# Splitting each 256-column product of the value phase into two of 128 columns

## The chip, the core and the metric

The kernel runs on one core of one Trainium2 chip. The metric is the time on the device in microseconds: the kernel before takes 3204.21 us, the median of three runs from 3204.08 to 3205.99. A difference of under 0.2% (6.4 us) counts here as no difference.

The core's engines work side by side, each with its own list of instructions: TensorE (PE in the profile) multiplies matrices, VectorE (DVE) and ScalarE (ACT) work on elements, GpSimd (POOL) and SyncE (SP) mostly start transfers. TensorE's work shows in two rows of the profile: a weight load (PEld) puts the stationary operand, here called the stationary block, into the array, and a matmul (PE) streams the moving operand past it. Results go to PSUM, memory beside the array in banks of 512 fp32 columns.

## The reference

Two attention blocks, one after the other, on a batch of 8 images of 512 channels and 32 x 32 positions (1024 tokens). All is fp32. One block, cut to what matters:

```python
xn  = group_norm(x, 8 groups) * gamma + beta
qkv = einsum('oc,bchw->bohw', qkv_w, xn) + qkv_b     # q, k, v: 512 channels each
attn = softmax(einsum('bhds,bhdt->bhst', q, k) * scale)   # 8 heads of 64
out = einsum('bhst,bhdt->bhds', attn, v)
x = x + einsum('oc,bchw->bohw', proj_w, out) + proj_b
```

The second block is the same with other weights. The change is in how `v` is computed.

## The kernel before, in words

The work is cut into 16 jobs: one image in one layer each. The images are taken in pairs, so that the two layers of an image are not neighbours. A job has four stages on TensorE, and the stages of neighbouring jobs are laced into one order that the kernel writes out itself (PE, ACT and DVE keep the order in which the Python code issues instructions; side work is issued by `later(delay, fn)` when a counted time, moved on by `advance(us)`, has come; this counted time is a plan, and nothing on the chip waits for it):

- **Value phase** (`v_phase`, line 482). It makes `v` with tokens on partitions. The 512 x 512 by 512 x 1024 product is done as one level of a seven-product scheme: the operands are cut into 2 x 2 blocks, sums and differences of blocks are formed (`tx` on the data side, `FACTOR` on the weight side), and seven block products replace eight. Each block product is 256 input channels by 512 tokens by 256 output channels.
- **Deep phases** (`deep_phases`, line 574). The output projection of the job before, then `k` and `q` of this job, with two levels of the scheme, 49 small products each, issued at line 636.
- **Attention** (`Attention`, line 858). 64 steps per job; each computes scores (line 878) and the product of the exponentials with `v` (line 909). Both address the array in quarters of 64 x 64.
- Group norm of a later job is laced in on ACT and DVE.

Inside the value phase, `group(i)` is called for `i` in 0 and 1: each takes half of the 512 tokens of a block product, that is two tiles `ti` of 128 tokens, and has four PSUM banks of its own (`z`, `y`, `u`, `v`). A bank holds two token tiles side by side, 256 output channels each. The function `one` (line 491) issues one product: the stationary block is a 128-channel by 128-token piece of the data, the moving operand is 256 columns of one weight block `w`. `product` calls it for two token tiles `ti` and two halves `cc` of the 256 input channels, so that a block product for one `i` is four calls. The second `cc` adds to the first in PSUM. `chain` (line 431) runs after each block product what empties or copies banks: `scalar.copy` at lines 438, 442, 518 and 522, `tensor_add` at line 520. `half_phase` issues all seven block products for `i` = 0 and 1 by turns. Only for the first job, `begin` issues the first half of some products earlier, between the steps of group norm; there, tiny products of one column (`averages` at line 329 and `variance` at line 341, for the group norm's statistics) stand between the products of line 494.

Per job this makes 7 x 2 x 2 x 2 = 56 calls of `one`; over 16 jobs, 896. In the trace each call stands as two passes, that is two weight loads and two matmul records of the same shape: 112 of each per job, 1792 of each in all. The same holds for every fp32 product of the kernel.

Of the flags: a product with `start` set begins an accumulation afresh; it is set only for the first product of a bank (`ti == 0`, `cc == 0`).

Of the kernel before, what the change touches and what calls it, by code (L numbers as in the profile page):

```python
# [19 lines left out]
P = 128  # L20
# [17 lines left out]
CH = C // 2  # L38
# [34 lines left out]
def fast_path(  # L73
# [10 lines left out]
    nc = tc.nc  # L84
# [8 lines left out]
    ps, turns = {}, [0]  # L93
# [116 lines left out]
    def wide(w):  # L210
        return w.rearrange("p a b -> p (a b)")[:, : 2 * CH].rearrange("p (cc o) -> p cc o", cc=2)
# [165 lines left out]
    xn, tx, to = [None], [None], [None]  # L377
# [15 lines left out]
    def right(src, t, o):  # L393

        if o in (4, 5, 6):
            return t[:, {5: 0, 6: 1, 4: 2}[o]]
        rows = 0 if o in (1, 7) else 2
        cols = slice(0, HALF) if o in (1, 2) else slice(HALF, S)
        return src[:, rows : rows + 2, cols]
# [54 lines left out]
    def half_phase(n, which, group, order):  # L454

        steps = []
        begins.clear()
        for i in range(2):
            by = {b: bank(i, b, f"{b}_{which}_{n}_{i}") for b in ("zyuv", "uvzy")[i]}
            product, put5, put, begin = group(i)  # L460
            steps.append(chain(product, put5, put, *(by[b] for b in "zyuv")))
            at = {1: by["z"], 5: by["v"], 2: by["y"]}
            begins.append(lambda o, begin=begin, at=at: begin(o, at[o]))
        thunks = []
        for o in order:
            key = (n, which, o)
            turns = (1, 0) if o == order[-1] and n > 0 else (0, 1)

            def first(o=o, i=turns[0]):
                steps[i](o)  # L470
                advance(1.72)

            def second(o=o, key=key, i=turns[1]):
                steps[i](o)
                if key in held:
                    used(key)
                advance(1.72)

            thunks += [first, second]
        return thunks  # L480

    def v_phase(n, order, first=None):
        vt[0] = acts.tile([P, NT, C], F32, tag="v", name=f"v_{n}")
        dst, src = vt[0], xn[0]

        def group(i):
            s5 = epool.tile([P, 2, HALF], F32, tag="e", name=f"s5_{n}_{i}")[:, 0, :]

            begun = []

            def one(o, ps, ti, cc, start):
                w = first[:, FACTOR[o]] if first is not None else wide(held[n, V, o])
                t0 = (2 * i + ti) * P
                nc.tensor.matmul(  # L494
                    ps[:, ti * CH : (ti + 1) * CH],
                    right(src, tx[0], o)[:, cc, t0 : t0 + P], w[:, cc, :],
                    start=(start and ti == 0 and cc == 0), stop=(cc == 1),
                    skip_group_check=True,
                )

            def begin(o, ps):
                one(o, ps, begun.count(o), 0, o in (1, 5))
                begun.append(o)

            def product(o, ps, start):
                for ti in range(2):
                    for cc in range(2):
                        if cc == 1 or o not in begun:
                            one(o, ps, ti, cc, start)

            def tokens(ps):
                return ps.rearrange("p (t c) -> p t c", t=2)

            def put(oh, sh, ps):
                t0 = sh * NT // 2 + 2 * i
                to_ = dst[:, t0 : t0 + 2, oh * CH : (oh + 1) * CH]
                if sh == 0:
                    nc.scalar.copy(to_, tokens(ps))  # L518
                else:
                    nc.vector.tensor_add(to_, tokens(ps), tokens(s5))  # L520

            return product, lambda ps: nc.scalar.copy(s5, ps), put, begin

        return half_phase(n, V, group, order)
# [253 lines left out]
    def last_weights(n):  # L778
        w = acts.tile([P, NW, 2, CH], F32, tag="deep", name="w_last")
        nc.sync.dma_start(w, factors[O, jobs[n][1]])  # L780
        return w
# [502 lines left out]
    for n in range(-1, len(jobs)):  # L1284
        last = n + 1 == len(jobs)
        outs = None
        if n >= 0:
# [7 lines left out]
            if last:  # L1295
                w = last_weights(n)
# [311 lines left out]
```

## Time and profile before

| What | Value |
|---|---|
| Median of three runs | 3204.21 us |
| Span of the profiled execution, first to last instruction | 3202.4 us |
| TensorE matmul records | 22917, busy 3183.5 us (99%) |
| Weight loads | 22917, busy 1862.2 us (58%) |
| VectorE | 2773.9 us (87%) |
| ScalarE | 1914.3 us (60%) |
| Mean granted TensorE clock | 0.999 |
| One value phase, first to last matmul start (jobs 3 to 16) | 24.49 us |

The profile is of one execution on the chip. The span lies 1.8 us below the median of the runs, which is time before the first and after the last instruction and the scatter of one execution. A matmul's row runs from the moment it begins to read to a modelled end, and rows overlap: the distance from one start to the next, not the row's length, tells what a pass costs. In the listings, "x16" merges sixteen neighbouring records of one kind, with the start of the first.

### The profile page before, as it was taken

What the parts mean: (1) busy time and instruction counts of PE and PEld (TensorE: products, weight loads), DVE (VectorE), ACT (ScalarE), POOL (GpSimd) and SP (SyncE); (2) the same over time, 40 slices, a digit from 0 to 9 for tenths busy, and PEclk for the clock granted to TensorE, in tenths of its full rate; (3) what the DMA queues carried; (4) which work ended last, traced back from release to release, by engine and by line L of the source; (5) the groups of instructions that cost most, each with busy time, mean ns of one, the idle gap of its engine ahead of it and who ended that gap; (6) DMA issues with size and microseconds to landing.
All of it is one profiled execution on the core that took longest, in us unless ns stands there. A gap on an engine that the chain in (4) does not pass through costs nothing.

```text
span 3202.4 us, 57786 instructions
## 1 busy us (share of the span) xinstructions
PE 3183.5 (99%) x22917; PEld 1862.2 (58%) x22917; DVE 2773.9 (87%) x3990; ACT 1914.3 (60%) x3063; POOL 99.5 (3%) x94
## 2 busy tenths in 40 slices
PE   9999999999999999999999999999999999999999
PEld 7366384663836648366483754837547375573744
DVE  8897999979889798897988889888898888978878
ACT  4746646466565665656656565565656656566564
POOL 0000000000000000000000000000000000000000
PEclk9999999999999999999999999999999999999999
DMA  8234172350713315034170421504316051150611
GB/s 291 74 105 123 49 216 67 95 166 22 213 25 90 89 28 158 22 105 130 31 211 16 117 69 37 149 16 137 101 44 194 16 138 48 49 136 16 174 37 42
DMA packets 156726, 307.80 MB, mean 96 GB/s; under 512 B 34088, under 2 KB 60576, under 8 KB 156192
## 3 DMA queue, kind: packets, MB, share of 16 engines
q1 hardware_dynamic: 139856, 272.05, 26.6%
q0 software_dynamic: 16592, 31.99, 6.1%
q8 instruction: 181, 2.97, 0.4%
q14 instruction: 97, 0.79, 0.1%
HBM read 225.13 MB, written 45.68 MB: 85 GB/s over the span
## 4 chain that ended last, share of the span: by engine, by line
PE 94%; DVE 5%; DMA 1%; issue 0%; ACT 0%; POOL 0%; DVEq 0%; SPq 0%; ACTq 0%; POOLq 0%
PE sc L878 27%; PE po L909 27%; PE zd L636 10%; PE vd L636 10%; PE z L494 6%; PE yd L636 5%; PE ud L636 4%; PE v L494 2%; PE y L494 2%; PE u L494 1%; DVE acc L895 1%; PE z_last L822 0%; DMA x<-p 0%; DMA w<-deep 0%; DVE w L156 0%
## 5 line engine op out<-in xcount | busy, mean ns | idle before, releaser
L883 ACT ACTIVATE e<-sc 128x1024 f32<-128x1024 f32 x1024 | 1045.0, 1024 | 563.6 <-PE sc L878 456.2
L878 PE MATMUL sc<-q,k 64*64 64x512 f32 x8192 | 1058.2, 589 | 0.0
L909 PE MATMUL po<-e,v 64*64 64x512 f32 x8192 | 1057.3, 589 | 0.0
L895 DVE TENSOR_TENSOR acc<-acc,e 128x1024 f32<-128x1024 f32 x768 | 936.2, 1219 | 58.7 <-ACT e L883 12.1
L909 PEld LDWEIGHTS po<-e,v 64*64 64x64 f32 x8192 | 313.2, 133 | 565.7 <-issue 552.9
L878 PEld LDWEIGHTS sc<-q,k 64*64 64x64 f32 x8192 | 311.6, 133 | 562.3 <-issue 544.2
L893 DVE TENSOR_TENSOR acc<-e,e 128x1024 f32<-128x1024 f32 x128 | 156.4, 1222 | 112.2 <-ACT e L883 112.1
L636 PE MATMUL zd<-deep,w 128*128 128x256 f32 x860 | 240.9, 379 | 1.1 <-DVE p L653 0.6
L636 PE MATMUL vd<-deep,w 128*128 128x256 f32 x804 | 224.4, 380 | 4.4 <-ACT yd L438 2.3
L636 PEld LDWEIGHTS zd<-deep,w 128*128 128x128 f32 x860 | 163.1, 190 | 24.7 <-DVE p L653 1.5
L636 PEld LDWEIGHTS vd<-deep,w 128*128 128x128 f32 x804 | 152.3, 190 | 27.2 <-ACT yd L438 2.7
L925 DVE TRANSPOSE_TENSOR_REDUCE r<-acc 128x32 f32<-128x1024 f32 x128 | 158.5, 1238 | 0.6
L682 POOL DMA_DIRECT2D x<-p x61 | 73.4, 1203 | 1974.0 <-ACT p L646 1408.5
L636 PE MATMUL vd<-os,w 128*128 128x256 f32 x420 | 118.2, 380 | 1.6 <-DVE p L655 1.5
L668 DVE TENSOR_TENSOR p<-p,p 128x1024 f32<-128x1024 f32 x94 | 114.2, 1215 | 0.0
L494 PE MATMUL z<-w,t 128*128 128x256 f32 x480 | 110.9, 379 | 0.0
L494 PE MATMUL z<-w,xn 128*128 128x256 f32 x480 | 110.1, 382 | 0.0
L518 ACT COPY v<-z 128x512 f32<-128x512 f32 x32 | 18.8, 586 | 148.7 <-PE z L494 148.7
L494 PEld LDWEIGHTS z<-w,xn 128*128 128x128 f32 x480 | 90.0, 190 | 23.8 <-issue 12.2
L442 ACT COPY ud<-zd 128x256 f32<-128x256 f32 x156 | 55.7, 357 | 76.5 <-PE zd L636 75.5
L653 DVE TENSOR_TENSOR p<-vd,s 128x256 f32<-128x256 f32 x63 | 26.7, 424 | 85.6 <-PE vd L636 85.6
L657 ACT COPY s<-vd 128x256 f32<-128x256 f32 x156 | 58.2, 373 | 70.1 <-PE vd L636 70.1
(242 smaller groups left out, 4193.8 us busy)
## 6 DMA issues: line engine op xcount, KB each, us to landing
w<-deep SPq DMA_DIRECT2D x287, 448.0 KB, 3.6
x<-p POOLq DMA_DIRECT2D x61, 512.0 KB, 6.5
rb<-rd SPq DMA_DIRECT2D x96, 256.0 KB, 4.1
w<-keep SPq DMA_DIRECT2D x84, 256.0 KB, 2.7
deep<-w SPq DMA_DIRECT2D x42, 448.0 KB, 3.3
w<-wqkv_dram SPq DMA_DIRECT2D x57, 256.0 KB, 2.8
x<-x_dram SPq DMA_DIRECT2D x28, 512.0 KB, 6.2
out_dram<-x SPq DMA_DIRECT2D x28, 512.0 KB, 6.0
```

What stands on the lines that cost most here:

```text
L442: nc.scalar.copy(u, z)
L494: nc.tensor.matmul(ps[:, ti * CH : (ti + 1) * CH], right(src, tx[0], o)[:, cc, t0 : t0 + P], w[:, cc, :], start=(start and ti == 0 and cc ...
L636: nc.tensor.matmul(ps, lhs[:, FACTOR[i], :], moving[i], start=start, stop=True, skip_group_check=True,)
L657: return chain(product, lambda ps: nc.scalar.copy(s5, ps), put, z, y, u, w)
L668: outer.append(lambda: nc.vector.tensor_add(to_, a, b))
L682: nc.gpsimd.dma_start(to_, p(part), accum_op=ALU.add)
L878: nc.tensor.matmul(sc[h * HD : (h + 1) * HD, j, :], k[r, hp, k0 : k0 + HD], q[r, hp, sh * HALF : (sh + 1) * HALF], start=True, stop=True,)
L883: nc.scalar.activation(e, sc, AF.Exp, scale=SCALE)
L893: nc.vector.tensor_add(acc[g], self.es[i - 1], e)
L895: nc.vector.tensor_add(acc[g], acc[g], e)
L909: nc.tensor.matmul(po[g][j * HD : (j + 1) * HD, h, :], v[r, kc, d0 : d0 + HD], e[r, j, :], start=(kc == 0), stop=(kc == NT - 1),)
L925: nc.vector.tensor_reduce(self.r[:, 0, m, :], self.acc.pop(g).rearrange("p j (b e) -> p (j b) e", e=RP), AX.X, ALU.add, apply_transpose=True,)
```

## The change

In `one`, the call of line 494 becomes a loop over two parts. Each part uses the same stationary block and takes 128 of the 256 columns of `w`, and writes 128 of the 256 columns of the bank's half. The flag `start` is set only for part 0.

```diff
-                nc.tensor.matmul(
-                    ps[:, ti * CH : (ti + 1) * CH],
-                    right(src, tx[0], o)[:, cc, t0 : t0 + P], w[:, cc, :],
-                    start=(start and ti == 0 and cc == 0), stop=(cc == 1),
-                    skip_group_check=True,
-                )
+                for part in range(2):
+                    c0 = part * P
+                    nc.tensor.matmul(
+                        ps[:, ti * CH + c0 : ti * CH + c0 + P],
+                        right(src, tx[0], o)[:, cc, t0 : t0 + P], w[:, cc, c0 : c0 + P],
+                        start=(start and ti == 0 and cc == 0 and part == 0), stop=(cc == 1),
+                        skip_group_check=True,
+                    )
```

`P` is 128, `CH` is 256. Nothing else differs; `advance(1.72)` for each block product, which paces the side work, is as before.

## The prediction

> **What bounds the kernel now.** I read the page's engine totals first, then the chain that ended last, then the order of time inside one value phase, and last the few places where the trace holds matmuls shorter than 256 columns.
>
> ```profile
> span 3202.4 us, 57786 instructions
> PE 3183.5 (99%) x22917; PEld 1862.2 (58%) x22917; DVE 2773.9 (87%) x3990; ACT 1914.3 (60%) x3063; POOL 99.5 (3%) x94
> ...
> PEclk9999999999999999999999999999999999999999
> ...
> PE 94%; DVE 5%; DMA 1%; issue 0%; ACT 0%; POOL 0%; DVEq 0%; SPq 0%; ACTq 0%; POOLq 0%
> ...
> L494 PE MATMUL z<-w,t 128*128 128x256 f32 x480 | 110.9, 379 | 0.0
> L494 PE MATMUL z<-w,xn 128*128 128x256 f32 x480 | 110.1, 382 | 0.0
> ...
> L494 PEld LDWEIGHTS z<-w,xn 128*128 128x128 f32 x480 | 90.0, 190 | 23.8 <-issue 12.2
> ```
>
> TensorE is busy from end to end at full clock and makes 94% of the chain, so any time added to its stream shows in full. The groups of line 494 have no idle time ahead of them. Loads equal matmuls in number (22917 each): every pass brings its own weight load. 190 ns is a load's row, 379 a matmul's, but both rows overlap their neighbours, so the cost must come from starts. The order of time in the third value phase, TensorE alone (start in us, row length in us, then the group):
>
> ```profile
> 398.72 3.62 PE L494 MATMUL v<-w,t 128*128 128x256 f32 x16
> 402.18 3.62 PE L494 MATMUL z<-w,t 128*128 128x256 f32 x16
> 405.63 3.62 PE L494 MATMUL y<-w,xn 128*128 128x256 f32 x16
> 409.08 3.62 PE L494 MATMUL z<-w,xn 128*128 128x256 f32 x16
> 412.54 3.62 PE L494 MATMUL u<-w,xn 128*128 128x256 f32 x16
> 415.99 1.89 PE L494 MATMUL z<-w,t 128*128 128x256 f32 x8
> ```
>
> Sixteen passes every 3.454 us: (415.99 - 398.72) / 80 = 215.9 ns a pass; the nanosecond records of the trace give 215.83. The view of waits, cut to this phase, has no TensorE wait. The phase is one unbroken stream, paced by the moving columns; each load starts 1 to 2 ns after the matmul before it and is hidden under that.
>
> What happens when the matmul is too short to hide the load shows only in the first job, where one-column products stand in the same stream:
>
> ```profile
> 15.47 0.28 PE L329 MATMUL pm<-mv,blk 128*128 128x1 f32 x2
> 15.61 1.11 PE L494 MATMUL v<-raw_v,t 128*128 128x256 f32 x4
> 16.56 0.28 PE L341 MATMUL pvar<-dev,blk 128*128 128x1 f32 x2
> 16.70 1.11 PE L494 MATMUL v<-raw_v,t 128*128 128x256 f32 x4
> 17.65 0.38 PE L1239 MATMUL first_u<-any 128*128 128x512 bf16 x1
> ```
>
> From 15.474 to 16.561 and on to 17.647 (the records' nanoseconds), each stretch holds two one-column passes and four of 256: 1.0865 us less 4 x 0.2158 leaves 223 ns, 111.6 ns for each short pass. A narrow cut shows the loads:
>
> ```profile
> 15.48 0.19 PEld L329 LDWEIGHTS pm<-mv,blk 128*128 128x128 f32 x1
> 15.59 0.30 PEld L494 LDWEIGHTS v<-raw_v,t 128*128 128x128 f32 x2
> ```
>
> In nanoseconds these loads start at 15.476, 15.586 and 15.697: 110 and 111 apart. The same distances at 12.4 and 16.6 us are 111 and 111, 110 and 112. So a pass which does nothing but bring its weights takes 110.8 (between loads) to 111.6 ns (between matmuls). That is the other pace of this engine.
>
> **What the Trainium skill says.** "TensorE: Matmul & The Clock Gate", section "Step-by-step: what each phase is for", says that the weights of the next tile load while the current matmul runs, into a background buffer. The trace agrees: 1 to 2 ns from matmul to load, and no lengthening of the 215.83 ns. Its section "LDWEIGHTS (loading the stationary operand)" prices a load at its columns over 1.2 GHz, 106.7 ns for 128; the trace's 110.8 is near, with the hand-off in it. Its section "Back-to-back issue gap" gives a bf16 matmul N/2.4 + 2.5 ns alone, but about 81 ns at N = 128 when each has its load, against 56 alone: 25 ns that overlap did not hide. No fp32 pair of 128 columns is in the trace before, so I keep this as the upper bound. "Perfetto Trace Analysis", section "Per-instruction lifecycle: what the profiler-reported window actually captures", says a TensorE row starts at prefetch and its end is estimated; hence starts alone are used here.
>
> **The change, part by part.** (1) Removed: 896 products, traced as 1792 passes at 215.83 ns. (2) Added: 1792 products, 3584 passes of 128 columns. Could the second part skip the load, its block being the same? The built program has full products, and in the trace before, the idle products of line 1130 use one block twice running and each pass still has its load. Besides, the two passes of one fp32 product sit between. I count 3584 loads.
>
> (3) Cost of a new pass, bounded from both sides. By columns: 256 columns take 215.83 ns; if 2.5 ns of it is fixed (the skill's figure), 128 take 106.7 + 2.5 = 109.2 ns. By load: 110.8 to 111.6. If both run side by side, as the first half of each matmul already does, the longer sets the pace: I take 111.0, inside the load's bounds. Two new passes cost 222.0 against 215.83: +6.2 ns for each old pass, x 1792 = +11.1 us, 0.69 us in each value phase. The lower end is 109.2: +2.6 x 1792 = +4.6 us. The upper end, 25 ns unhidden on 109.2, is 134: +52.6 x 1792 = +94 us.
>
> (4) Issue: a pair of load and matmul every 111 ns is an instruction per 55.5. Attention already does that for whole stages:
>
> ```profile
> 300.64 1.04 PE L878 MATMUL sc<-q,k 64*64 64x512 f32 x8
> 301.50 1.04 PE L909 MATMUL po<-e,v 64*64 64x512 f32 x8
> 302.36 1.04 PE L878 MATMUL sc<-q,k 64*64 64x512 f32 x8
> ```
>
> Eight matmuls and their eight loads every 0.86 us are 53.6 to 53.8 ns an instruction, so the sequencer keeps up. The margin is thin: the view proves this pace and no faster one.
>
> (5) Waits: the built program keeps the order of DVE, ACT, POOL and SP unchanged, and TensorE has 180 waiting products at this line before and after; no wait or signal is added. Nothing is moved past a queue. DMA: none. Behind TensorE, the copies at lines 438, 442, 518, 520 and 522 are released 0.1 us later per product; they wait for TensorE now (ACT for line 518 alone 185.4 us), so only the next TensorE stage matters, and it stands behind the same stream. DVE's side work in the phase (23.4 of 24.9 us busy) gets 0.7 us more room; if it were late, its cost would come at the deep phases, where TensorE waits 9 us in all today. One recovery: in the second value phase TensorE waits 1.2 us for the attention's last sum (line 932); the 24 old passes before it are slower now and take back 24 x 6.2 ns, 0.15 us. The first phase's half clock until 12.3 us doubles a handful of passes, both old and new. Sum: +11.0 us. Against the profiled span: 3202.4 + 11.0 = 3213.4; the 1.8 us that the median has over it stay: **3215.2 us**.
>
> **The rivals.**
> - *Column pace* (ends on the other side: no change). If the load's 1.6 ns start-up and hand-off vanish under a matmul of equal length, a pass is 109.2 ns: +4.6, 3208.8 us. For it: each path alone would fit. Against: one-column passes leave the load nothing to wait for and still pace at 111. It decides below (215.83 + 6.4/1.792) / 2 = 109.7 ns; above this the change is measurably slower.
> - *Partial exposure.* Load and matmul now end together, so a small hand-off that today has 105 ns of slack could show: 112.5 to 124 ns a pass, where 124 is two instructions at the 62 ns that the skill's clock-gate page ("Wait — 56ns, not 53.3ns?") gives for a software-decoded matmul. +16 to +58 us: 3221 to 3262. Against: attention's 53.6 ns per instruction and the even 110 to 112 chain.
> - *Load not hidden*, 134 ns: 3298 us. Against: today's loads are hidden wholly; for: the skill's 81 against 56.
> - *Load skipped*: even then columns pace at 109.2, the first rival's time. Nothing in the profile offers a gain above 0.2%, since all columns still stream; only a stage shifting by luck remains.
>
> **How the numbers follow.** Load pace (110 to 112.5 ns, 3210.6 to 3220): 0.60. Column pace, skipped load included: 0.16. Partial exposure: 0.14. Unhidden: 0.08. A gain: 0.02. The likeliest gives 3215.2. The range takes load and column pace (0.76) from 3207, and the lower half of partial exposure, to 3241 (0.83). 0.2%, 6.4 us, is what a measurement can tell: slower is 0.60 + 0.14 + 0.08 = 0.82, same 0.16, faster 0.02.
>
> **What would show it.** Right: 3584 loads at the line; starts in a value phase 110.5 to 111.5 ns apart, so a block product's row of 32 passes every 3.55 us and a phase of 25.1 to 25.2 us; weight loads nearly touching; no TensorE wait in the phase; attention and deep phases as before. Column pace: 3.49 us a block product. Exposure: 3.6 us and more. Wrong also if loads stay at 1792, if starts jitter (issue), or if TensorE waits grow in the deep phases.

## The result and the profile after

The changed kernel takes 3216.21 us, the median of five runs from 3215.82 to 3217.89, against 3204.21: a ratio of 1.0037 with a 95% interval of 1.0023 to 1.0051. Run again later with four runs of its own it came to 1.0052 (1.0035 to 1.0069). It is slower by some 12 to 16 us, against 11 forecast; both intervals lie above the 0.2% that counts as a difference.

The page of the kernel after, its totals, the line of the clock, the chain and two of the groups (busy us and mean ns behind the bar, then idle time):

```profile
span 3214.4 us, 61370 instructions
...
PE 3196.8 (99%) x24709; PEld 1926.0 (60%) x24709; DVE 2775.1 (86%) x3990; ACT 1912.8 (60%) x3063; POOL 99.5 (3%) x94
...
PEclk9999999999999999999999999999999999999999
...
PE 94%; DVE 4%; DMA 1%; issue 0%; SPq 0%; ACT 0%; DVEq 0%; ACTq 0%
...
L496 PEld LDWEIGHTS z<-w,xn 128*128 128x128 f32 x960 | 109.5, 192 | 12.2 <-issue 12.2
L496 PE MATMUL z<-w,t 128*128 128x128 f32 x960 | 114.5, 276 | 0.0
```

TensorE has 24709 matmuls and as many loads, 1792 of each more than before: no load was skipped. The span grew by 12.0 us and TensorE's busy time by 13.3; VectorE and ScalarE changed by at most 1.5 us. The chain is the same but for one per cent of VectorE. In the group of loads, the idle time was 23.8 us and is now 12.2, which is the one gap ahead of each phase, 0.76 us on average: the loads, which used to leave room between them, now follow each other without a break.

The order of time in the third value phase, TensorE alone:

```profile
398.30 3.74 PE L496 MATMUL v<-w,t 128*128 128x128 f32 x32
401.87 3.74 PE L496 MATMUL z<-w,t 128*128 128x128 f32 x32
405.44 3.74 PE L496 MATMUL y<-w,xn 128*128 128x128 f32 x32
409.02 3.74 PE L496 MATMUL z<-w,xn 128*128 128x128 f32 x32
412.59 3.74 PE L496 MATMUL u<-w,xn 128*128 128x128 f32 x32
416.17 1.95 PE L496 MATMUL z<-w,t 128*128 128x128 f32 x16
```

A block product took 3.454 us and takes 3.574: (416.17 - 398.30) / 160 = 111.7 ns a pass, 111.66 from the records' nanoseconds. From its first to its last matmul start the phase takes 25.43 us, against 24.49. No TensorE wait stands in it, as before. The busy time of the line's rows in this phase (stretch and its length, then TensorE, loads, clock, share of the DMA engines and GB/s), first of the kernel before, then of the kernel after:

```profile
395.10:419.70 24.60, 24.27 (x112) 21.20 (x112) 1.00 0.37 113
```

```profile
394.60:420.10 25.50, 25.21 (x224) 25.21 (x224) 1.00 0.34 109
```

Before, loads were busy for less time than matmuls; now both are busy for the same 25.21 us. From the sixth to the last job the period of a job is 197.85 us before and 198.69 after, in each of two traces of either kernel: +0.84 us, which is 112 x (2 x 111.66 - 215.83). Sixteen times that is 13.4 us. As the period grew by exactly this, the other stages of these jobs take what they took before.

### The profile page after: what moved, and what is told of

It is laid out like the page before. It is cut to its first block, busy times and chain, and to the rows that moved or that the text cites. A ratio compares the mean times of both kernels' runs of the same rounds, so it can differ in the third digit from the quotient of the medians.

```text
span 3214.4 us, 61370 instructions
## 1 busy us (share of the span) xinstructions
PE 3196.8 (99%) x24709; PEld 1926.0 (60%) x24709; DVE 2775.1 (86%) x3990; ACT 1912.8 (60%) x3063; POOL 99.5 (3%) x94
## 4 chain that ended last, share of the span: by engine, by line
PE 94%; DVE 4%; DMA 1%; issue 0%; SPq 0%; ACT 0%; DVEq 0%; ACTq 0%
PE sc L880 27%; PE po L911 27%; PE vd L638 10%; PE zd L638 10%; PE z L496 6%; PE yd L638 5%; PE ud L638 4%; PE y L496 2%; PE v L496 2%; PE u L496 1%; DVE acc L897 0%; PE z_last L824 0%; DMA w<-deep 0%; DMA x<-p 0%; DVE w L156 0%
## 5 line engine op out<-in xcount | busy, mean ns | idle before, releaser
L638 PEld LDWEIGHTS vd<-deep,w 128*128 128x128 f32 x804 | 152.7, 190 | 25.1 <-DVE p L657 2.5
L496 PEld LDWEIGHTS z<-w,xn 128*128 128x128 f32 x960 | 109.5, 192 | 12.2 <-issue 12.2
L496 PE MATMUL z<-w,t 128*128 128x128 f32 x960 | 114.5, 276 | 0.0
L496 PE MATMUL z<-w,xn 128*128 128x128 f32 x960 | 113.7, 277 | 0.0
L496 PEld LDWEIGHTS z<-w,t 128*128 128x128 f32 x960 | 112.0, 192 | 0.8
```

Of the source, the lines that this page charges most:

```text
L496: nc.tensor.matmul(ps[:, ti * CH + c0 : ti * CH + c0 + P], right(src, tx[0], o)[:, cc, t0 : t0 + P], w[:, cc, c0 : c0 + P], start=(start a ...
L638: nc.tensor.matmul(ps, lhs[:, FACTOR[i], :], moving[i], start=start, stop=True, skip_group_check=True,)
```

## The experiments

The theory that stands behind the forecast: **load pace**. A pass takes the longer of its columns and its weight load with the hand-off. The rivals: a pure **column pace** with a larger fixed part for each pass (5 ns instead of 2.5 gives 111.7 for 128 columns too, so the result alone does not exclude it), and **issue**, 55.8 ns for each of the two instructions of a pass.

### Another cut: 192 and 64 columns

Against the kernel after; the slices that follow end at `c1`, and `start` is set for `c0 == 0`:

```diff
-                for part in range(2):
-                    c0 = part * P
+                for c0, c1 in ((0, 192), (192, 256)):
```

> The 256 columns are cut into 192 and 64 instead of 128 and 128; the number of products, loads and columns is that of the change. Theory A (load pace: a pass takes the longer of its columns and about 111.6 ns for its weight load with the hand-off): the 192 part is paced by columns, 160 + 2.5 = 162.5 ns, the 64 part by its load, 111.6 ns; 274.1 against 215.83 for an old pass, +58.3 x 1792 = +104 us, about 3307 us, and two distances between matmul starts, 162 and 112, in the value phases. Theory B (column pace with a larger fixed part of about 5 ns for each pass): 256 columns are 213.3 + 2 x 5 = 223.3 ns however they are cut, so the time of the change, about 3216 us, with distances of 165 and 58 ns. Theory C (issue: 55.8 ns for each instruction, whatever it loads) gives the same as A here; the ladder tells A from C.

Measured: 3313.78 us against 3205.14, ratio 1.0339 (1.0322 to 1.0356), +109 us. The period of a job is 204.39 us: (204.39 - 197.85) / 112 = 58.4 ns for each old pass, where 58.3 was expected. Column pace is out: the same count of products, loads and columns costs eight times as much when it is cut unevenly. The single distances between matmul starts are not those expected: they run 56, 112, 218, 163 and not 112, 112, 162, 162. Their sum, 549, is twice 274.5, and the starts of the loads have the expected distances: 110, 112, 164, 162. So the row of a short matmul starts ahead of its turn, and where passes of different length follow each other, loads or the sum of a whole cycle tell the cost of a pass, not single distances between matmuls.

The first value phase is longer than the rest, 41.9 us from first to last start against 31.1 (in the kernel before 27.6 against 24.5), which is more than enough for the 5 us above the forecast. Two stretches of the trace show why in the column of the clock, which is the last but two:

```profile
8.70:50.70 42.00, 40.50 (x224) 40.08 (x224) 0.76 0.63 216
203.50:234.70 31.20, 30.78 (x224) 30.83 (x224) 1.00 0.18 55
```

The array ran at half clock from 8.0 to 28.4 us; in the kernel before from 8.9 to 12.3.

### Four parts of 64 columns

Against the kernel after, with the same slices:

```diff
-                for part in range(2):
-                    c0 = part * P
+                for c0, c1 in ((0, 64), (64, 128), (128, 192), (192, 256)):
```

> Four parts of 64 columns each. Theory A (load pace): four passes of 111.6 ns, 446.4 against 215.83 for an old pass, +230.6 x 1792 = +413 us, about 3617 us; distances of 111 to 112 ns only. Theory B (columns with 5 ns fixed): 213.3 + 4 x 5 = 233.3, +31 us, 3235 us. Theory C (issue): as A.

Measured: 3661.89 us, ratio 1.1427 (1.1408 to 1.1446), +457 us. Every later value phase is 50.395 us from first to last start and its distances are 111 and 112 ns: 64 columns take as long as 128, and the period of a job, 223.71 us, gives (223.71 - 197.85) / 112 = 230.9 ns for each old pass, 230.6 expected. The second value phase, in the columns of the views above, has twice as many passes as with 128 columns in twice the time:

```profile
263.00:314.00 51.00, 50.35 (x448) 50.26 (x448) 1.00 0.18 58
```

The 44 us above the forecast are in the first value phase alone, 98.7 us: its passes stand 213 to 214 ns apart, almost twice the pace of all later ones. The trace's record of the full clock begins only at 112.9 us, 4.9 us after the deep phases with their 256 columns have started. So the mechanism holds and the forecast left out the start's clock.

### The deep phases split instead

Against the kernel before:

```diff
             def product(i, ps, start):
-                nc.tensor.matmul(
-                    ps, lhs[:, FACTOR[i], :], moving[i], start=start, stop=True,
-                    skip_group_check=True,
-                )
+                for c0 in (0, P):
+                    nc.tensor.matmul(
+                        ps[:, c0 : c0 + P], lhs[:, FACTOR[i], :], moving[i][:, c0 : c0 + P],
+                        start=start and c0 == 0, stop=True, skip_group_check=True,
+                    )
```

> The value phase is as before; instead the 2303 products of the deep phases (4606 passes of 256 columns) are cut into two parts of 128 columns. If the load pace is a property of the pass and not of the value phase, each old pass costs 2 x 111.66 - 215.83 = 7.5 ns more: +34.5 us, about 3239 us. The deep phases hold some 9 us of TensorE waits today, of which the slower stream may take back a part, at most to +26 us. If the value phase's cost came from something of its own (its banks, its copies, one stationary block kept for two parts of one wide bank), the deep phases would be dearer or cheaper than that by more than 10 us.

Measured: 3236.97 us, ratio 1.0099 (1.0083 to 1.0116), +32 us (27 to 37). The period of a job is 200.06 us in most jobs: (200.06 - 197.85) / 294 = 7.5 ns for each of the 294 old passes that the deep phases of a job have, as in the value phase. The value phase has nothing of its own: a pass of another stage, with other banks and readers, pays the same. The groups of that line carry it, and a small wait remains at its old place:

```profile
L637 PE MATMUL zd<-deep,w 128*128 128x128 f32 x1720 | 247.4, 275 | 0.7 <-DVE p L654 0.5 <-DVE p L656 0.2
L637 PEld LDWEIGHTS zd<-deep,w 128*128 128x128 f32 x1720 | 219.1, 192 | 1.5 <-DVE p L654 0.9 <-DVE p L656 0.6
```

The idle time of these loads fell from 24.7 us to 1.5, the same sign as in the value phase. That the whole is 2 to 3 us below 34.5 would fit slack in TensorE's waits in the first jobs, but lies inside the interval.

### A ladder of widths

Against the kernel before; the call, behind the last product, is left out here:

```diff
+    def ladder():
+        ps = bank(0, "y", "ladder")
+        half = env.blk.bitcast(BF16)
+        def series(block, moving, rows, cols):
+            for _ in range(40):
+                nc.tensor.matmul(ps[:rows, :cols], block, moving, start=True, stop=True)
+        two = env.blk.unsqueeze(1).to_broadcast([P, 2, P])
+        series(env.blk, two, P, 2 * P)
+        series(env.blk, env.blk, P, P)
+        series(env.blk, env.blk[:, :HD], P, HD)
+        series(env.blk, env.blk[:, :RP], P, RP)
+        series(env.blk[:, :HD], env.blk, HD, P)
+        series(env.blk[:, :HD], env.blk[:, :HD], HD, HD)
+        series(half[:, :P], half, P, 2 * P)
+        series(half[:, :P], half[:, :P], P, P)
+        series(half[:, :P], half[:, :HD], P, HD)
```

> The kernel before, with nine series of 40 products each put after its last product, all into one bank that nothing reads, all from one stationary block. Widths are given as columns of the block / moving columns. Start-to-start distances of a pass in ns. Theory A (load pace): fp32 128/256: 215.8; 128/128: 111.6; 128/64: 111.6; 128/32: 111.6; with 64 columns in the block, 64/128: 109 (columns now decide), 64/64: about 58 (half a load, or 64 columns, 53.3 plus 3 to 5). Theory C (issue, 55.8 ns for each instruction): 64/64 stays at 111.6, and 64/128 at 111.6. Theory B (columns with 5 ns fixed): 128/64: 58, 128/32: 32. If a load of the block already in the array were skipped, 128/64 would fall to 56. The bf16 series (one pass for each product, half the time for each column): 256 columns 109.2; 128 columns between 56 (load hidden) and 81; 64 columns shows the bf16 load's own pace, 30 to 60.

Measured, start to start of a pass at full clock (from the nanosecond records; the typical step, or the mean where one clock held for the whole series):

| Type | Block columns | Moving columns | ns a pass | What it shows |
|---|---|---|---|---|
| fp32 | 128 | 256 | 215.8 | columns pace |
| fp32 | 128 | 128 | 111.6 | load pace |
| fp32 | 128 | 64 | 111.7 (111 and 112) | load pace |
| fp32 | 128 | 32 | 111 and 112 | load pace |
| fp32 | 64 | 128 | 109.2 | columns pace again |
| fp32 | 64 | 64 | 58.3 | load pace of half a block |
| bf16 | 128 | 256 | 109.2 | columns pace |
| bf16 | 128 | 128 | 55.8 | columns pace, load hidden |
| bf16 | 128 | 64 | 29.2 | columns pace, load hidden |

Busy time and, in brackets, the passes of each series in a cut of the trace (the fourth row is 32 moving columns, the fifth the block of 64 columns with 128, the sixth 64 with 64):

```profile
3198.00:3206.00 8.00, 8.00 (x39) 7.04 (x38) 1.00 0.11 37
3214.00:3222.00 8.00, 8.00 (x74) 8.00 (x74) 1.00 0.01 2
3223.00:3231.00 8.00, 8.00 (x74) 8.00 (x73) 1.00 0.00 0
3232.00:3236.00 4.00, 4.00 (x39) 4.00 (x38) 1.00 0.01 4
3250.50:3255.50 5.00, 5.00 (x48) 5.00 (x47) 1.00 0.00 0
3257.00:3260.00 3.00, 3.00 (x55) 3.00 (x54) 1.00 0.00 0
```

A cut counts every row that reaches into it, two to four rows more than its length divided by the pace. What the reader is to see: 74 passes in 8 us for 128 and for 64 columns. Loads that are busy throughout are no proof of load pace by themselves: they are so in the fifth row too, where columns pace, because the row of a load is longer than the time it costs (192 ns against 111.6 for a block of 128 columns). Issue falls by the sixth row: the two instructions of a pass come every 58 ns there, every 29 in the last bf16 series, so 111.6 is not their limit. Column pace falls by the third and fourth. Nor is it the width of the block as such that takes 111.6 ns: the last bf16 series has a block of 128 columns too and takes 29.2. And all series use one block again and again, and every pass has its load, 600 in all: an fp32 pass does not keep what it has.

The numbers give a form for the load: 128 columns 111.6, 64 columns 58.3, a difference of 53.3 for 64 columns; so a line through these two points is 0.833 ns a column plus 5 ns. That is the price in the Trainium skill's "TensorE: Matmul & The Clock Gate", section "LDWEIGHTS (loading the stationary operand)", columns over 1.2 GHz, with a hand-off of 5 ns on it. For bf16 that price does not fit: the load of a 128-column block hides behind a pass of 29.2 ns here. Moving columns cost, from 215.8 ns at 256 and 109.2 at 128, also 0.833 ns a column, plus 2.5.

### Half-width loads inside the kernel

Against the four-part kernel:

```diff
                 for c0, c1 in ((0, 64), (64, 128), (128, 192), (192, 256)):
+                    m = P if cc == 0 else HD
                     nc.tensor.matmul(
-                        ps[:, ti * CH + c0 : ti * CH + c1],
-                        right(src, tx[0], o)[:, cc, t0 : t0 + P], w[:, cc, c0:c1],
+                        ps[:m, ti * CH + c0 : ti * CH + c1],
+                        right(src, tx[0], o)[:, cc, t0 : t0 + m], w[:, cc, c0:c1],
```

> As the four-part kernel, 7168 products-passes at the line, but every product of the second half of the input channels (cc = 1) uses a block of 64 tokens instead of 128, so that 64 of the 128 tokens lack that half of their sum. The same number of instructions and of columns streamed, half of the loads at half width. Load pace: passes with the full block 111.6 ns, with the half block 58.3 (the ladder's 64/64); for an old pass 4 x (111.6 + 58.3) / 2 = 339.8 against 446.4, so 106.6 x 1792 = 191 us less than the four-part kernel: about 3471 us, some tens less if the first value phase leaves the half clock sooner. If the number of instructions or of passes set the pace, the four-part kernel's 3662 us stay.

Measured: 3556.39 us (two runs), 106 us less than the four-part kernel and not 191. The pace of each kind of pass is as expected: distances of 58 and 59 ns in the half-width runs, 111 and 112 in the full ones. What was left out is the change between widths. In one cycle at 1110 us the first load at half width starts 204 ns after the last matmul at full width (1111.078 to 1111.282), where 56 ns pass within the full-width run; the first load at full width starts 150 ns after the last matmul at half width (1111.740 to 1111.890), where 3 ns pass within the half-width run. The cycle of 16 passes is 1643 ns; 8 x 111.6 + 8 x 58.3 is 1359; 284 ns go into the two changes, 142 each on average. 28 cycles in a phase make that 8.0 us, of the 11.9 us that the forecast had for a phase. The ladder has one such change at full clock, from 64 columns in fp32 to 128 in bf16, and there too the load starts 150 ns after the last matmul. With the changes in it a later value phase takes 46.29 us instead of 50.40, which makes 62 us for fifteen of them, and the first takes 56.3 instead of 98.7, because the full clock comes sooner: 42 more, 104 of the 106. The skill's "TensorEngine Tiling (Array Packing)", section "Key Properties", says that a change of the tiling mode drains TensorE. The two gaps fit that; that they are this drain was not tested apart. The load's width sets the pace inside the kernel too: the number of passes and instructions and the columns streamed are the same as with four parts.

### Both kernels once more

No edit.

> The changed kernel again, unaltered. 3215 to 3217 us. If the 1.0 us that the wait of a product in the second deep phase for the copy at line 438 gave back, and the earlier end of the half clock (10.3 against 12.3 us), come from the change, both stand here again; if they are scatter of the start, they do not.

> The kernel before again, unaltered, for a second trace of it. 3203 to 3207 us. Same question from the other side: does the wait of 2.25 us in the second deep phase for the copy at line 438 come again, or was it scatter of one execution.

Measured: 3220.47 us (3217.95 to 3222.45) for the changed kernel, above what was expected, and 3204.99 for the kernel before. The period of a job in its trace is the 198.69 us of the first, so the excess is not in the repeated part; its trace is that of the fastest of the four runs, and what the others lost stays open. Spans 3216.2 and 3203.2: +13.0. TensorE's waits in the second trace of the kernel before and of the kernel after (us in total, times, longest):

```profile
PE vd L636 <- ACT yd L438: 2.2, 1, 2.2
...
PE v L494 <- DVE q L932: 1.4, 1, 1.4
```

```profile
PE vd L638 <- ACT yd L438: 2.2, 1, 2.2
...
PE vd L638 <- DMA w<-deep: 0.9, 1, 0.9
...
PE v L496 <- DVE q L934: 0.6, 1, 0.6
```

The long wait behind line 438 is in both: that it was 1.2 us instead of 2.2 in the first trace after is scatter and no gift of the change. So is the half clock at the start: it ended at 12.3 and 14.7 us before, 10.3 and 14.8 after. Two things repeat in both pairs. The wait in the second value phase is shorter: 1.2 and 1.4 us before, 0.8 and 0.6 after. And a wait for a weight transfer in the deep phases of the fourth job (0.0 to 0.2 us before) becomes 0.9 to 1.1. It stands where the images of the next pair are loaded (line 219) in the same queue; what makes that transfer late was not tested and stays open, at about 1 us.

## Why the prediction was right

**What bounds.** TensorE's stream did, and all that was added to it showed: 13.4 us from the phases, 12.0 and 13.0 between spans. That 3216.2 came within 1 us of 3215.2 is in part luck: the cost of the passes was 2.3 us above the forecast, and in that execution the wait behind line 438 happened to be 1 us short. The later runs of the same kernel lie at 3217.95 to 3222.45.

**Step 2, the loads.** 3584 were counted and made. The ladder shows that even one block used for forty products is loaded for every pass.

**Step 3, the cost of a pass.** The choice between the two paces was right and the term a little small: 111.0 was taken, 111.66 measured, 7.5 ns for each old pass against 6.2, 13.4 us against 11.1. It lies just outside the 110.5 to 111.5 that was named as the sign. The phase of 25.1 to 25.2 us was worked out a little short as well: between first and last start one must also count that the last pass starts 0.10 us later when the passes are half as long, so 111.0 ns means 25.3; 25.43 was measured. And in the chances the lower edge of load pace, 3210.6 us, is the line of 0.2%; 110 ns would be 3211.7. The better reading was already in the trace before: the 111.6 between matmuls, worked out from the one-column products, is the number that came; the 110.8 between loads, taken into the mean, was counted from a first load that begins as much as 2 ns behind its matmul (15.476 against 15.474). The hand-off is 5 ns and not 4.

**Step 4, issue.** Right, and with more margin than attention could show: 58 ns for a pair in fp32, 29 in bf16.

**Step 5, waits.** No wait inside the phase, right. The recovery in the second value phase was put at 0.15 us; the traces show 0.4 to 0.8, with a scatter of 0.2. A wait for a transfer in the fourth job's deep phases, 0.9 to 1.1 us, was not foreseen.

**The rivals.** Column pace failed by 2.5 ns a pass: 109.2 against 111.7. A block of 64 columns does show it, 109.2. That made the difference between no change and a measurable one, since 109.7 was the point of decision. Partial exposure beyond the load's own pace was not there. The load not hidden, 134 ns, was taken from the 81 ns for a bf16 pair of 128 columns in the skill's "TensorE: Matmul & The Clock Gate", section "Back-to-back issue gap"; in the ladder, with one block used again and again, that pair takes 55.8, wholly hidden. Where the page and the measurement differ, the measurement decides.

## What to carry to other kernels

In this kernel and in the ladder each fp32 pass brings its weight load, and the load of a 128-column block takes 111.6 ns. By estimate, moving columns hide it only from about 131 columns on ((111.6 - 2.5) / 0.833 = 131, from the ladder's figures; no width between 128 and 192 was run). Splitting 256 columns into equal halves lies just below that point and costs 3.5% of the stage; an uneven cut or a finer one pays the full load for every short piece. Before splitting a product, look in the trace for the shortest matmul beside a full load: what it takes, counted over a whole stretch because short rows start ahead of their turn, is the floor.

## What was not expected

**Narrow passes do not raise the clock, and very narrow ones lose it.** The half clock that stands in the first value phase ended at 10.3 and 14.8 us with 128 columns, as before the change (12.3 and 14.7), at 28.4 with 192 and 64, and at 32.7 with four parts and half of the loads at half width. With four parts of 64 columns it stayed until 112.9 us, though TensorE's rows were busy for 97.2 of that phase's 98.7 us, and it ended 4.9 us after the wider passes of the deep phases had begun. Later phases of the same 64-column passes kept full clock for 50 us. In the ladder, passes of 32 columns, which began at 3231.6 us, lost it at 3236.2, and it came back at 3249.8 in the series of 64-column blocks with 128 moving columns, which had begun at 3244.6. Rows were back to back in nearly all of this, so an open row is not what keeps the clock up. The cases stand in the order of the share of time in which columns stream at the full-clock pace, an estimate from the paces above: 96% with 128 columns, 78% with 192 and 64, 52% with half of the loads at half width, 48% with 64 and 24% with 32. That this share is what decides is not shown, nor where the threshold lies. With 192 and 64 columns the clock was halved once more, from 264.0 to 267.4 us, behind a TensorE wait of 2.1 us for the copy at line 438; the kernel before has a wait of 2.25 us there and kept its clock.

**A change of block width costs 142 ns** on top of the passes, the mean of both directions, more than a whole pass of 111.6 ns.
